# A second layer's condition computed with features on partitions: the adapters become the held operand, the squares are summed by a product with ones, and the normed rows are no longer transposed

## The chip, the core and the metric

The kernel runs on one core of a Trainium2 chip. The metric is the device time of one execution in microseconds (us). Five engines work beside each other, each through its own queue: TensorE (PE; its weight loads are listed as PEld), VectorE (DVE), ScalarE (ACT), GpSimd (POOL) and SyncE (SP, which here only issues transfers).

## The reference, cut to what matters

The input x has 8 groups of 128 rows with 512 features. Two layers are added to it one after the other, each a condition followed by a gated feed-forward block. Layer 0's condition is a base product with low-rank experts, and its block has 4-bit weights. Layer 1 is where most of the change lies:

```python
def _L1_cond_ref(x, weight, adapter_ids):
    w = weight[adapter_ids]                     # (8, 512, 512): one adapter for each group
    return jnp.einsum('bsi,boi->bso', x, w)

def _L1_ffn_ref(x, ln_w, gate_w, up_w, down_w):
    var = jnp.mean(jnp.square(x), axis=-1, keepdims=True)
    nx = x * jax.lax.rsqrt(var + RMS_EPS) * ln_w
    g = jnp.einsum('bsh,ih->bsi', nx, gate_w)
    u = jnp.einsum('bsh,ih->bsi', nx, up_w)
    return jnp.einsum('bsi,hi->bsh', jax.nn.silu(g) * u, down_w)

x = x + _L0_ffn_ref(_L0_cond_ref(x, ...), ...)
x = x + _L1_ffn_ref(_L1_cond_ref(x, L1_cond_weight, itok_B_3_7), ...)
```

For each of the 8 groups b, a (128 x 512) block of rows is multiplied by that group's own 512 x 512 adapter; every row is divided by its root mean square; every feature is multiplied by its weight `ln_w`; and the result is the input of 1792 gate and 1792 up columns.

## The kernel before, in words

All activations are kept with features on partitions: `xT` is 128 partitions x 4 chunks (KC) x 1024 rows. The gate, up and down products of both layers take their activations in that form. They don't run in plain float32: each operand is split into a high part, a low part and a scaled difference, written as float32r, and three cheaper products are added. For the activations of layer 1 these three are `a3[0]` (hi), `a3[1]` (lo) and `a3[2]` (di).

The condition of layer 1 does run in plain float32. `adapt(b)` (L995) computes group b with rows on partitions: `xT` is the held operand (lhsT), the adapter, 512 columns at a time, is streamed, and four products add up to 128 rows x 512 features in one bank of PSUM. A plain float32 product shows as two records of PE and two of PEld. ACT squares the bank and sums along the free axis in the same instruction (L1008; the sum shows as an ACTIVATION_READ_ACCUMULATOR record), takes the root of the 128 x 1 result (L1009), DVE inverts it (L1010) and multiplies the bank with it (L1012, `nx`). `normed(b, nx)` (L1015) then has TensorE turn the four 128 x 128 pieces (L1019, a product against the identity), DVE multiplies by `ln_w` on the way out of PSUM (L1023, `raw`), ACT writes the high part (L1030), and DVE the low part (L1031) and the difference (L1032).

The loop over the 8 groups calls `adapt(b)` and then `normed(b - 1)`. These instructions are not in a hand-written order: the framework's scheduler orders each engine's queue by the order of the program and by what it takes to be ready. The adapters are fetched by gathers on POOL's queue, 1 MB each, into three buffers; the fetch of group b + 3 is released by group b's last product. The preparation of the first two chunks of gate and up weights (L940, L943 on ACT; L949, L952 on DVE) is issued just before the loop.

What follows, and layer 0, is in a fixed order (`manual_schedule`): ACT, DVE and TensorE take their instructions as written. A small planner decides while the program is written which engine gets what. It keeps a clock that advances 0.2326 us for each product, and for ACT and DVE a time to which each is booked (`load`). `rescale` (L174) puts a pass over a PSUM bank on the engine whose booking would end earlier, and waiting tasks (weight preparation, splitting of h) are put in where they fit:

```python
def took(engine, n):
    return 0.1 + n / 1000 if engine == "act" else 0.15 + n / 950
...
engine = min(load, key=lambda e: max(load[e], clock[0] + AFTER) + took(e, n))
```

The first chunk of layer 1's gate and up products (`gate_up`, L1081) works on the first 512 rows alone; the last group's `normed` is issued in its middle, after the products of the first of the three parts (which = (2,)) and before the other two (which = (0, 1)), because groups 4 to 7 are needed only when the second 512 rows come. A gate or up bank is rescaled (L179 on ACT, L181 on DVE) between these two.

The activation tables: Sqrt and Silu are in different tables, so there is one table load (L1044) after the last root. After the layer's first rows there is also a one-row product that decides a flag (`judge`, L813), issued in the first `normed`.

Of the kernel before, what the change touches and what calls it, by code (L numbers as in the profile page):

```python
# [13 lines left out]
F32 = mybir.dt.float32  # L14
# [5 lines left out]
AF = mybir.ActivationFunctionType  # L20
ALU = mybir.AluOpType

P = 128
B, T, D = 8, 128, 512
# [4 lines left out]
KC = D // P  # L29
# [66 lines left out]
def network_in(ctx, tc, a, out, by_groups, flag, again):  # L96
    nc = tc.nc
# [4 lines left out]
    def pair(name):  # L102
        return psum.tile([P, 2, 512], F32, tag="ps", name=name)

    def bank(name):
        return pair(name)[:, 0, :]
# [15 lines left out]
    def behind(inst, other):  # L122

        info = mybir.DependencyInfo(mybir.DependencyClass.NoSync, mybir.DependencyReason.SCHED_ONLY)
        tc.add_manual_dep(inst.ins, other.ins.name, info, reason="order")
# [327 lines left out]
    def by_groups_of_scales():  # L453
# [243 lines left out]
        with tc.manual_schedule(engines={EngineType.PE, EngineType.DVE, EngineType.Activation}):  # L697
# [77 lines left out]
                for j in range(*pair0):  # L775
                    flush(f"w{j}")

            load["act"], load["dve"] = clock[0] + 1.0, clock[0] + 2.0

            queue_down(*BLOCKS0[0], "d0", at=clock[0] + 7.0)  # L780
            gate_up_pair(0, 1)
# [210 lines left out]

    last_root = [None]

    def adapt(b):  # L995
        ps = bank("adapt")
        wt = w1s.pop(b)
        for c in range(KC):
            nc.tensor.matmul(  # L999
                ps,  # L1000
                lhsT=xT[:, c, b * T : (b + 1) * T],
                rhs=wt[:, c * D : (c + 1) * D],
                start=(c == 0),
                stop=(c == KC - 1),
            )
        sq = ad.tile([P, D], F32, tag="t0", bufs=2, name="sq")
        ss = ad.tile([P, 1], F32, tag="ss", bufs=3, name="ss")
        nc.scalar.activation(sq, ps, AF.Square, accum_out=ss)  # L1008
        last_root[0] = nc.scalar.activation(ss, ss, AF.Sqrt, bias=eps, scale=1.0 / D)  # L1009
        nc.vector.reciprocal(ss, ss)  # L1010
        nx = ad.tile([P, D], F32, tag="t1", bufs=2, name="nx")
        nc.vector.tensor_scalar(nx, ps, ss, None, ALU.mult)  # L1012
        return nx

    def normed(b, nx):  # L1015
        both = pair("nxT")
        pt = both[:, 0, :]
        for c in range(KC):
            nc.tensor.transpose(pt[:, c * T : (c + 1) * T], nx[:, c * P : (c + 1) * P], ident)  # L1019
        if judges:  # L1020
            judges.pop()(both[:, 1, :])
        raw = ad.tile([P, KC, T], F32, tag="raw", bufs=2, name="raw")
        nc.vector.tensor_tensor(  # L1023
            raw,
            pt.rearrange("p (c t) -> p c t", c=KC),
            ln_w[:, :, None].to_broadcast([P, KC, T]),
            ALU.mult,
        )
        hi, lo, di = (x[:, :, b * T : (b + 1) * T] for x in a3)
        nc.scalar.activation(hi, raw, AF.Copy, scale=HSCALE)  # L1030
        nc.vector.tensor_tensor(lo, raw, hi.bitcast(F32), ALU.subtract)  # L1031
        nc.vector.scalar_tensor_tensor(  # L1032
            di, lo.bitcast(F32), -1.0 / EPS, hi.bitcast(F32), ALU.mult, ALU.add
        )

    prev = None
    for b in range(B):
        nx = adapt(b)
        if b + 3 < B:
            load_w1(b + 3)  # L1040
        if prev is not None:
            normed(b - 1, prev)
        prev = nx
    behind(nc.scalar.activation(root, root, AF.Silu), last_root[0])  # L1044


    w1_stack.close()
    f1 = ctx.enter_context(tc.tile_pool(name="f1", bufs=1, side="right"))
    load["act"], load["dve"] = clock[0] + 2.0, clock[0] + 1.0
    d3, h3 = {}, {}  # L1050

    def gu_sums(ps, j, half, tb, which):
# [132 lines left out]
    with tc.manual_schedule(engines={EngineType.PE, EngineType.DVE, EngineType.Activation}):  # L1185
        for j0, j1 in BLOCKS1:
            for j in range(j0, j1):
                if j + 2 < NJ1:
                    flush(f"w{j + 1}")
                    prepare(j + 2, f"w{j + 2}")  # L1190
                    if j + 4 < NJ1:
                        load_wgu(j + 4)
                flush(f"w{j}")
                if j == 0:

                    two = [begin_chunk(i) for i in range(2)]
                    first, second = slice(0, 1), slice(1, 2)
                    gate_up(two[0], first, between=lambda: normed(B - 1, prev))
                    ad_stack.close()
                    fd = ctx.enter_context(tc.tile_pool(name="fd", bufs=1, side="left"))  # L1200
                    gate_up(two[1], first)
                    gate_up(two[0], second)
                elif j == 1:
                    gate_up(two[1], second)
                else:
                    flush(f"h{j - 2}")
                    gate_up(begin_chunk(j))
                if j == max(j0, 1):
                    prepare_down(load_down(j0, j1))
            flush("down")  # L1210
            for j in range(j0, j1):
                flush(f"h{j}")
            if j1 == NJ1 and by_groups:

                again.append(nc.values_load(flag[:1, :], min_val=0, max_val=1))
                tc.mark_branch_hint_location("again", hint=again[0], engines=FETCHED)
            down(j0, j1)
# [158 lines left out]
```

## Time and profile before

| | |
|---|---|
| median of 3 runs | 436.3 us (435.57 to 436.6) |
| profiled execution | 436.83 us |
| its span, first to last instruction | 434.9 us |
| mean granted TensorE clock | 0.996 of full speed |
| busy: PE, PEld, DVE, ACT, POOL | 424.8, 334.5, 302.4, 232.0, 9.0 us |
| first adapt product (L999) to first layer-1 gate product (L1056) | 165.80 to 197.36 us |
| adapt products, 64 records | 28.9 us busy, 592 ns median of one |
| transposes (L1019), 32 records | 4.9 us busy, 272 ns median of one |

A line of a timeline gives: start in us from the beginning of the span, duration in us, engine, line of the program, instruction, written tile <- read tiles, shape (for a product: rows*columns of the held operand, then the streamed shape), count, and in brackets how long the engine was idle before and what ended that. Products of TensorE are pipelined: the duration of one includes its way through the array, so the pace is read from the distance between starts, not from durations. In the chain that ended last each share is the part of the span that a line or an engine carries on the way back from the last instruction.

### The profile page before, as it was taken

How to read it: one execution, taken by the hardware profiler on the slowest of the kernel's cores; microseconds unless marked ns; L12 is line 12 of the kernel's file. 1: busy time of each engine (PE TensorE's matmuls, PEld its weight loads, DVE VectorE, ACT ScalarE, POOL GpSimd, SP SyncE). 2: the span in 40 equal slices, each digit the busy share in tenths (PEclk: the TensorE clock that was granted, in tenths of full speed). 3: DMA queues.
4: the chain of work that ended last, by engine and by line, in shares of the span. 5: the costliest groups of instructions: out<-in, count | busy, mean ns of one | idle time of the engine just before them, and what ended most of it. 6: DMA issues, size and time to landing. Idle time of an engine off the chain costs nothing.

```text
span 434.9 us, 4847 instructions
## 1 busy us (share of the span) xinstructions
PE 424.8 (98%) x1855; PEld 334.5 (77%) x1855; DVE 302.4 (70%) x432; ACT 232.0 (53%) x269; POOL 9.0 (2%) x20
## 2 busy tenths in 40 slices
PE   8999999999999999999999999999999999999992
PEld 8875778888888764447888888888888888888882
DVE  3998979998998769768179634679334676725552
ACT  5923899678877765347478132484132471425420
POOL 1000000000002001100000000000000000000000
PEclk9999999999999999999999999999999999999998
DMA  8931301010001505842114101132001110000013
GB/s 290 344 150 49 98 0 50 18 37 2 0 2 48 242 6 204 301 167 83 64 50 145 48 2 48 50 97 72 2 0 48 50 48 26 0 0 2 2 53 146
DMA packets 12094, 33.07 MB, mean 76 GB/s; under 512 B 1568, under 2 KB 4256, under 8 KB 11040
## 3 DMA queue, kind: packets, MB, share of 16 engines
q1 hardware_dynamic: 9760, 22.21, 15.3%
q0 software_dynamic: 1152, 8.39, 5.1%
q10 hardware_dynamic: 1152, 2.10, 1.3%
q8 instruction: 16, 0.26, 0.2%
q14 instruction: 14, 0.11, 0.1%
HBM read 30.59 MB, written 2.10 MB: 75 GB/s over the span
## 4 chain that ended last, share of the span: by engine, by line
PE 91%; DVE 4%; DMA 2%; ACT 1%; issue 0%; SPq 0%; ACTq 0%; DVEq 0%
PE gate L1056 18%; PE up L1056 18%; PE down L1121 17%; PE gate L539 9%; PE down L587 8%; PE up L539 8%; PE base L390 5%; PE adapt L999 5%; PE base L416 2%; DMA xb<-in_xb 2%; PE experts L293 1%; DVE xT L599 1%; PE nxT L1019 1%; ACT sl L555 1%; DVE h L558 1%; DVE w L952 1%
## 5 line engine op out<-in xcount | busy, mean ns | idle before, releaser
L1056 PE MATMUL gate<-a,w 128*128 128x512 f32 x336 | 81.8, 390 | 0.0
L1056 PE MATMUL up<-a,w 128*128 128x512 f32 x336 | 81.4, 389 | 0.0
L1121 PE MATMUL down<-h,d 128*128 128x512 f32 x336 | 76.8, 389 | 0.0
L1056 PEld LDWEIGHTS up<-a,w 128*128 128x128 f32 x336 | 63.1, 188 | 13.2
L1121 PEld LDWEIGHTS down<-h,d 128*128 128x128 f32 x336 | 63.1, 188 | 13.1
L1056 PEld LDWEIGHTS gate<-a,w 128*128 128x128 f32 x336 | 62.7, 188 | 13.5 <-ACT gate L179 0.6
L1073 DVE SCALAR_TENSOR_TENSOR h<-up,sl 128x1024 f32<-128x1024 f32 (+1 forms) x16 | 17.5, 1092 | 51.0 <-PE up L1056 44.6
L539 PE MATMUL gate<-a,dq 128*128 128x512 f32 (+1 forms) x176 | 47.7, 393 | 0.1
L539 PE MATMUL up<-a,dq 128*128 128x512 f32 (+1 forms) x176 | 47.4, 391 | 0.0
L587 PE MATMUL down<-h,wd 128*128 128x512 f32 (+1 forms) x176 | 42.3, 393 | 0.6 <-DVE h L193 0.4
L587 PEld LDWEIGHTS down<-h,wd 128*128 128x128 f32 (+1 forms) x176 | 32.5, 188 | 9.5 <-DVE h L193 0.9
L539 PEld LDWEIGHTS gate<-a,dq 128*128 128x128 f32 (+1 forms) x176 | 32.4, 185 | 8.4 <-ACT sl L555 0.6
L539 PEld LDWEIGHTS up<-a,dq 128*128 128x128 f32 (+1 forms) x176 | 32.4, 185 | 7.9 <-DVE a L671 0.3
L203 ACT ACTIVATE h<-h 128x1024 fp32r<-128x1024 f32 (+1 forms) x25 | 26.4, 1054 | 15.9 <-DVE h L1073 15.5
L1070 ACT ACTIVATE sl<-gate 128x1024 f32<-128x1024 f32 (+1 forms) x16 | 14.7, 919 | 35.8 <-PE gate L1056 35.8
L193 DVE TENSOR_TENSOR h<-h,h 128x1024 fp32r<-128x1024 f32 (+1 forms) x25 | 30.5, 1218 | 3.4 <-ACT h L203 3.4
L179 ACT ACTIVATE gate<-gate,ratio 128x1024 f32<-128x1024 f32 (+1 forms) x24 | 26.1, 1086 | 10.6 <-PE gate L539 10.6
L179 ACT ACTIVATE gate<-gate 128x1024 f32<-128x1024 f32 (+1 forms) x15 | 13.8, 923 | 30.8 <-PE gate L1056 30.8
L999 PE MATMUL adapt<-w,xT 128*128 128x512 f32 x64 | 28.9, 597 | 0.0
L179 ACT ACTIVATE down<-down 128x1024 f32<-128x1024 f32 (+1 forms) x10 | 9.2, 923 | 35.8 <-PE down L1121 35.8
L179 ACT ACTIVATE up<-up,ratio 128x1024 f32<-128x1024 f32 (+1 forms) x23 | 25.0, 1085 | 4.9 <-PE up L539 4.9
L1138 DVE SCALAR_TENSOR_TENSOR xT<-down,xT 128x1024 f32<-128x1024 f32 (+1 forms) x17 | 19.6, 1161 | 9.3 <-PE down L1121 9.1
(137 smaller groups left out, 482.6 us busy)
## 6 DMA issues: line engine op xcount, KB each, us to landing
wgu<-in_wgu SPq DMA_DIRECT2D x14, 512.0 KB, 3.3
wd<-in_wd SPq DMA_DIRECT2D x6, 512.0 KB, 3.7
qw<-in_qw_gu SPq DMA_DIRECT2D x5, 512.0 KB, 4.2
xT<-in_xT SPq DMA_DIRECT2D x2, 1024.0 KB, 11.6
xb<-in_xb ACTq DMA_DIRECT2D x4, 256.0 KB, 5.6
xb<-in_xb SPq DMA_DIRECT2D x4, 256.0 KB, 6.1
wT<-in_WT SPq DMA_DIRECT2D x4, 256.0 KB, 5.9
qwd<-in_qw_d SPq DMA_DIRECT2D x2, 512.0 KB, 8.2
```

Of the source, the lines that this page charges most:

```text
L179: nc.scalar.activation(ps, ps, AF.Copy, scale=by)
L193: nc.vector.tensor_tensor(lo, x, hi.bitcast(F32), ALU.subtract)
L203: nc.scalar.activation(hi, x, AF.Copy, scale=HSCALE)
L390: nc.tensor.matmul(base[m], lhsT=wT3[i][:, m, c * P : (c + 1) * P], rhs=x_parts(tb)[i][:, c, :], start=(i == 0 and c == 0), stop=(i == 1 a ...
L539: nc.tensor.matmul(ps, lhsT=dqs[j][:, c, half, :], rhs=a3[i][:, c, tb * TB : (tb + 1) * TB], start=(c == 0 and i == 0), stop=(i == 1), ski ...
L587: nc.tensor.matmul(ps[:, tb], lhsT=wds[k][:n, m * P : (m + 1) * P], rhs=h2[k][i][:, tb], start=(first and i == 0), stop=(i == 1), skip_gro ...
L999: nc.tensor.matmul(ps, lhsT=xT[:, c, b * T : (b + 1) * T], rhs=wt[:, c * D : (c + 1) * D], start=(c == 0), stop=(c == KC - 1),)
L1056: nc.tensor.matmul(ps, lhsT=w3[j][i][:, c, half * P : (half + 1) * P], rhs=a3[i][:, c, tb * TB : (tb + 1) * TB], start=(i == 2 and c == 0) ...
L1070: nc.scalar.activation(sl, ps, AF.Silu, scale=1.0 + EPS)
L1073: nc.vector.scalar_tensor_tensor(h, ps, 1.0 + EPS, sl, ALU.mult, ALU.mult)
L1121: nc.tensor.matmul(banks[m, tb], lhsT=d3[j][i][:, m * P : (m + 1) * P], rhs=h3[j][i][:, tb], start=(i == 0 and j == j0), stop=(j == j1 - 1 ...
L1138: nc.vector.scalar_tensor_tensor(x, ps, -EPS, x, ALU.mult, ALU.add)
```

## The change

The condition of layer 1 is computed in the turned form at once. For each of the four 128-feature pieces m of the output, a 128 x 128 piece of the adapter is held and the group's 128 rows of `xT` are streamed, over four chunks c: 16 products of 128 columns in place of 4 of 512. The bank then holds features on partitions, 4 pieces x 128 rows, and needs no transposes. The sum of squares now runs over partitions and pieces: ACT squares the bank (no accumulator), DVE adds the four pieces (a strided `tensor_reduce`, 128 x 512 to 128 x 128), and TensorE multiplies the result with a 128 x 128 matrix of ones, which gives every partition the full sum for each row (`mean`, in the second bank of the same pair). Root and reciprocal are now taken of 128 x 128 elements. `ln_w` is per partition and goes into four scaled copies on ACT (`y`), and DVE multiplies `y` in place by the inverse root. High part, low part and difference are as before.

The mean, root and reciprocal of group b - 1 (`rooted`) are issued in the middle of group b's products, after two of its four pieces. For the last group `rooted`, the table load and `normed` are issued together in the middle of the first gate and up chunk. Two starting values of the planner's bookings change: ACT's at the start of layer 0's gate and up products from 1.0 to 2.0, DVE's at the start of layer 1's from 1.0 to 2.0.

```diff
-            load["act"], load["dve"] = clock[0] + 1.0, clock[0] + 2.0
+            load["act"], load["dve"] = clock[0] + 2.0, clock[0] + 2.0
...
-    def adapt(b):
-        ps = bank("adapt")
+    all_ones = ad.tile([P, P], F32, name="all_ones")
+    nc.gpsimd.memset(all_ones, 1.0)
+
+    def adapt(b, between):
+        both = pair("adapt")
+        ps = both[:, 0, :]
         wt = w1s.pop(b)
-        for c in range(KC):
-            nc.tensor.matmul(
-                ps,
-                lhsT=xT[:, c, b * T : (b + 1) * T],
-                rhs=wt[:, c * D : (c + 1) * D],
-                start=(c == 0),
-                stop=(c == KC - 1),
-            )
+        roots = None
+        for m in range(KC):
+            if m == KC // 2 and between is not None:
+                roots = between()
+            for c in range(KC):
+                nc.tensor.matmul(
+                    ps[:, m * T : (m + 1) * T],
+                    lhsT=wt[:, c * D + m * P : c * D + (m + 1) * P],
+                    rhs=xT[:, c, b * T : (b + 1) * T],
+                    start=(c == 0),
+                    stop=(c == KC - 1),
+                )
         sq = ad.tile([P, D], F32, tag="t0", bufs=2, name="sq")
-        ss = ad.tile([P, 1], F32, tag="ss", bufs=3, name="ss")
-        nc.scalar.activation(sq, ps, AF.Square, accum_out=ss)
-        last_root[0] = nc.scalar.activation(ss, ss, AF.Sqrt, bias=eps, scale=1.0 / D)
-        nc.vector.reciprocal(ss, ss)
-        nx = ad.tile([P, D], F32, tag="t1", bufs=2, name="nx")
-        nc.vector.tensor_scalar(nx, ps, ss, None, ALU.mult)
-        return nx
-
-    def normed(b, nx):
-        both = pair("nxT")
-        pt = both[:, 0, :]
-        for c in range(KC):
-            nc.tensor.transpose(pt[:, c * T : (c + 1) * T], nx[:, c * P : (c + 1) * P], ident)
+        ss = ad.tile([P, T], F32, tag="ss", bufs=2, name="ss")
+        y = ad.tile([P, KC, T], F32, tag="y", bufs=2, name="y")
+        nc.scalar.activation(sq, ps, AF.Square)
+        nc.vector.tensor_reduce(ss, sq.rearrange("p (m t) -> p t m", m=KC), mybir.AxisListType.X, ALU.add)
+        for m in range(KC):
+            nc.scalar.activation(y[:, m, :], ps[:, m * T : (m + 1) * T], AF.Copy, scale=ln_w[:, m : m + 1])
+        return (both, ss, y), roots
+
+    def rooted(got):
+        both, ss, _ = got
+        mean = both[:, 1, :T]
+        nc.tensor.matmul(mean, lhsT=all_ones, rhs=ss, start=True, stop=True)
         if judges:
-            judges.pop()(both[:, 1, :])
-        raw = ad.tile([P, KC, T], F32, tag="raw", bufs=2, name="raw")
-        nc.vector.tensor_tensor(
-            raw,
-            pt.rearrange("p (c t) -> p c t", c=KC),
-            ln_w[:, :, None].to_broadcast([P, KC, T]),
-            ALU.mult,
-        )
+            judges.pop()(both[:, 1, T:])
+        rms = ad.tile([P, T], F32, tag="rms", bufs=2, name="rms")
+        last_root[0] = nc.scalar.activation(rms, mean, AF.Sqrt, bias=eps, scale=1.0 / D)
+        nc.vector.reciprocal(rms, rms)
+        return rms
+
+    def normed(b, got, rms):
+        raw = got[2]
+        nc.vector.tensor_tensor(raw, raw, rms[:, None, :].to_broadcast([P, KC, T]), ALU.mult)
         hi, lo, di = (x[:, :, b * T : (b + 1) * T] for x in a3)
...
     for b in range(B):
-        nx = adapt(b)
+        got, rms = adapt(b, None if prev is None else lambda: rooted(prev))
         if b + 3 < B:
             load_w1(b + 3)
         if prev is not None:
-            normed(b - 1, prev)
-        prev = nx
-    behind(nc.scalar.activation(root, root, AF.Silu), last_root[0])
+            normed(b - 1, prev, rms)
+        prev = got
+
+    def last_row():
+        rms = rooted(prev)
+        behind(nc.scalar.activation(root, root, AF.Silu), last_root[0])
+        normed(B - 1, prev, rms)
...
-    load["act"], load["dve"] = clock[0] + 2.0, clock[0] + 1.0
+    load["act"], load["dve"] = clock[0] + 2.0, clock[0] + 2.0
...
-                    gate_up(two[0], first, between=lambda: normed(B - 1, prev))
+                    gate_up(two[0], first, between=last_row)
```

## The prediction

> **What bounds the kernel now.** I read the page first (engine shares, the chain that ended last), then the order of time around the rows of the condition, then single lines for durations.
>
> ```profile
> PE 424.8 (98%) x1855; PEld 334.5 (77%) x1855; DVE 302.4 (70%) x432; ACT 232.0 (53%) x269; POOL 9.0 (2%) x20
> PE 91%; DVE 4%; DMA 2%; ACT 1%; issue 0%; SPq 0%; ACTq 0%; DVEq 0%
> ```
>
> TensorE is the bound: it carries 91% of the chain. A microsecond of product taken away on it is worth one, unless a new wait takes its place. One steady row of the condition:
>
> ```profile
> 181.34 0.60 PE L1019 MATMUL nxT<-ident,nx 128*128 128x128 f32 x4
> 181.54 0.60 ACT L1008 ACTIVATE sq<-adapt 128x512 f32<-128x512 f32 x1 [2.08 <-PE adapt L999]
> 181.77 3.60 PE L999 MATMUL adapt<-w,xT 128*128 128x512 f32 x8
> 181.97 0.69 DVE L1023 TENSOR_TENSOR raw<-nxT,small 128x512 f32<-128x512 f32 x1 [0.99 <-PE nxT L1019]
> 182.03 0.20 ACT L1008 ACTIVATION_READ_ACCUMULATOR sq<-adapt 128x1 f32 x1
> 182.26 0.29 ACT L1009 ACTIVATE ss<-ss,eps 128x1 f32<-128x1 f32 x1
> 182.59 0.16 DVE L1010 RECIPROCAL ss<-ss 128x1 f32<-128x1 f32 x1
> 182.70 0.63 ACT L1030 ACTIVATE a<-raw 128x512 fp32r<-128x512 f32 x1
> 182.79 0.75 DVE L1012 TENSOR_SCALAR nx<-adapt,ss 128x512 f32<-128x512 f32 x1
> 183.45 0.68 DVE L1031 TENSOR_TENSOR a<-raw,a 128x512 fp32r<-128x512 f32 x1
> 184.17 0.69 DVE L1032 SCALAR_TENSOR_TENSOR a<-a,a 128x512 fp32r<-128x512 f32 x1
> 185.21 0.60 PE L1019 MATMUL nxT<-ident,nx 128*128 128x128 f32 x4
> ```
>
> From transposes to transposes a row lasts 3.87 us: 8 product records at 0.430 (3.44) and 4 transposes at 0.1075 (0.43). TensorE doesn't wait in it. DVE works 0.16+0.75+0.69+0.68+0.69 = 2.97 us of it, ACT 0.60+0.19+0.29+0.63 = 1.71. So 0.9 us a row is spare on DVE and 2.2 on ACT.
>
> Where the rows end and the gate and up products begin (first chunk):
>
> ```profile
> 200.74 0.63 ACT L1030 ACTIVATE a<-raw 128x512 fp32r<-128x512 f32 x1
> 201.28 1.05 ACT L940 ACTIVATE w<-wgu 128x1024 fp32r<-128x1024 f32 x1
> 202.23 0.57 ACT L1070 ACTIVATE sl<-gate 128x512 f32<-128x512 f32 x1
> 202.71 1.05 ACT L943 ACTIVATE wgu<-wgu 128x1024 f32<-128x1024 f32 x1
> 204.79 0.58 ACT L179 ACTIVATE gate<-gate 128x512 f32<-128x512 f32 x1 [1.04 <-PE gate L1056]
> 205.50 2.04 PE L1056 MATMUL gate<-a,w 128*128 128x512 f32 x8
> ```
>
> ACT goes here in the written order: the last row's high part (200.74), the next weights (201.28), the Silu, their second pass, then the gate rescale that TensorE needs for its products at 205.50. ACT had 1.04 us to spare before that rescale. Whatever makes the last row's high part over about 1 us later stops TensorE.
>
> **The change, part by part.**
>
> *Products.* Eight records of 512 columns become 32 of 128 a row; four transposes become two records of the mean. The streamed columns are the same (8x512 = 32x128). The price of a 128-column record is bounded by two rows: the transposes, 0.1075, and
>
> ```profile
> 8.25 4.90 PE L293 MATMUL experts<-wa,xb 128*128 128x136 f32 x40 [0.29 <-DMA xb<-in_xb]
> 12.90 0.48 PE L390 MATMUL base<-a,wT 128*128 128x512 f32 x1
> ```
>
> 40 records of 136 columns between 8.25 and 12.90, 0.116 each, every one with its own full-size weight load, as after the change. I take the experts row, the nearer in kind, times 128/136: 0.109. A row then costs 34x0.109 = 3.71 us against 3.87, 0.16 less; 3.66 to 3.94 by the two ends. Eight rows: -1.3 us (-1.7 to +0.6).
>
> The Trainium skill ("TensorE: Matmul & The Clock Gate", Back-to-back issue gap) speaks against the change: in a stream where every product has its own weight load, both set the spacing, about 81 ns where the product alone needs 56 at 128 columns. An estimate that stretches 0.1075 by that ratio has 0.156 a record, 5.3 us a row and some 11 us lost. The experts row, at 0.116 with loads between all its products, says otherwise.
>
> *DVE.* Gone: the norm multiply from PSUM (0.75) and the one-column reciprocal (0.16). New: a reduction over 512 elements, and a reciprocal over 128. The reduction's rows are 0.25 us for 93 elements (L693) and 0.68 for a 512-element pass (L1031); I take 0.69. Its strided read is in no row; I keep 0.6 to 1.2. For the reciprocal:
>
> ```profile
> L534 DVE RECIPROCAL ratio<-ratio x1: 566/566/566, 38.6 to 38.6; 128x66 f32<-128x66 f32 x1
> L534 DVE RECIPROCAL ratio_d<-ratio_d x1: 379/379/379, 41.8 to 41.8; 128x36 f32<-128x36 f32 x1
> ```
>
> 187 ns for 30 elements, 6.2 ns each: 128 cost 0.379+92x0.0062 = 0.95 us. DVE's row becomes 0.69+0.95+0.69+0.68+0.69 = 3.70 us, equal to TensorE's 3.71. The spare 0.9 us is gone.
>
> *ACT.* The square keeps 0.60 and loses its accumulator read (0.19). Four scaled copies of 128 columns come: the immediate-scale form is 0.58 at 512 and 1.01 at 1024 columns (L179), so 0.26 at 128; the pointer-scale form is 0.08 dearer (1.09 at 1024): 0.34, four make 1.36. The root grows from 1 to 128 elements: 0.29+127x0.00083 = 0.40. With the high part 0.63: 2.99 us a row. This hides under 3.71 while the order lets it; uncovered, the copies cost their 1.36.
>
> *The new wait.* TensorE now waits in the middle of each row for the reduction of the row before: 0.20 (product to ACT) + 0.60 + 0.05 + 0.69 + 0.06 = 1.60 us after that row's end, against a half row of 1.75. Behind the mean stand all further products. 0.15 us of slack is less than any DVE instruction (0.64 to 0.95) that happens to be ahead of the reduction. If DVE, at 3.70 plus three hand-offs of 0.05, sets the pace, it is 0.14 a row, 1.1 us; if TensorE needs only the reductions and DVE's rest may lag, nothing. I take +0.6 us.
>
> *First row.* DVE is in weight preparation until 171.25 (L949), so the first mean is possible at about 172.0; before, the first transposes waited as well (173.22 instead of 172.93). Nothing, from -0.3 to +1.
>
> *Last row.* Let E be the end of the last adapt products. Now (E = 197.01) the last high part ends at 201.37, 4.4 after. After the change: square to E+0.8, copies to 2.16, the gate rescale (moved to ACT, below) to 2.74, then the root (the mean is done at 1.82+0.22) to 3.14. The table load and its dummy, 1.28+0.20, end at 4.62, under DVE's reciprocal and multiply; these two end at 3.2+0.95+0.69 = 4.84 if DVE is free, about 6.5 if it still has row 6's 1.6 us. So the high part ends between 5.5 and 7.2. From there 1.05+0.57+1.05+0.58 = 3.25 us of ACT to the end of the gate rescale: E+8.8 to 10.4. TensorE without a stall wants it at E + 1.82 + 0.22 + 3.64 + 1.82 = E+7.5. The stall is 1.3 to 2.9; now it is 205.50 - 197.01 - 8.14 = 0.35 (8.14 being the products and two sets of transposes). Net +1.0 to +2.6; I take +2.3, since row 6's work does stand ahead now too (its last two parts run at 201.95 and 202.67).
>
> *The planner's constants.* Layer 1: by its own costs the gate rescale was 1.92 on DVE and 2.61 on ACT, and is now 2.69 and 2.61; so gate goes to ACT and up to DVE, the reverse of before (counted above). Layer 0: with ACT booked one later, the first "up" goes to DVE (3.91 against 4.25) and ACT has eight rescales of the first pair instead of nine. TensorE's only stalls there are 0.34 us at 45.84 and 0.56 at 58.06, both of other causes; the planner's books meet again in the second pair. Nothing, -0.2 to +0.3. The ones tile is set by idle POOL.
>
> *Sum.* -1.3 products, +0.6 row waits, 0 first row, +2.3 last row, 0 planner: +1.6 us. On the profiled execution (span 434.9, 436.83 with the 1.93 around it) that is 438.4; its own time stands 0.5 above the median of the runs, 436.3, so the median goes to 437.9.
>
> **The rivals.**
> 1. *Faster: the waits hide.* If the copies of the first half run during the second half of the products, ACT is 0.7 us earlier at the end and the high part ends near E+5.0; the last-row stall is 0.75, net +0.4. With no row waits: -1.3+0.4 = -0.9, with the cheap record -1.3: 435.0 to 435.4. For it: 2.2 us of ACT were spare, DVE idles later (2.45 us before 209.47). Against: DVE at 3.70. It decides where the last high part ends before about E+5.2.
> 2. *Much slower: DVE is held in the written order*, reciprocal, reduction, multiply, then a wait for the high part (0.05+0.63+0.07), low part, difference: 3.70+0.75 = 4.45 a row, +0.58 on seven rows = 4.1, with the last row's 2.3: 442.7. Half of the rows so: about 440. For it: low and difference need the high part, which now queues behind four copies. Against: before, the scheduler moved the multiply (181.97) ahead of the next reciprocal.
> 3. *Adapter loads late.* The gathers are issued 0.5 us after a row's end and land in 5.4 to 7.3; two rows from now are 7.6. At most 0.2 a row, 1 us in all: about 438.5.
>
> **How the numbers follow.** The forecast, 436.7 to 439.5, has 0.47; rival 1 0.32; rival 2 0.16; rival 3 0.05. A difference of 0.2%, 0.9 us, is about what can be told from no change. Of the forecast 0.07 lies within it, of rival 1 0.05; so faster 0.27, same 0.12, slower 0.61. The range has to reach into rival 1 and half of rival 2: 434.9 to 441.0.
>
> **What would show it.** Right: adapt records near 0.109 apart, reciprocal near 0.95, gate rescale on ACT, and a TensorE wait of over 1 us ahead of the second chunk's gate products. Wrong: a reciprocal under 0.4 us (then DVE has its slack back), records at 0.15, or no wait there.

## The result, and the profile after

The changed kernel takes 440.17 us (median of 6 runs, 439.05 to 441.66) against 436.41 us for the kernel before (6 runs): the ratio is 1.0083, with a 95% interval of 1.0069 to 1.0097. It is 3.8 us slower, where 1.6 was forecast. The profiled execution took 439.05 us with a span of 437.3, the shortest of its six runs.

From the page of the changed kernel: busy time by engine, and the engines' shares of the chain that ended last.

```profile
PE 425.4 (97%) x2031; PEld 349.9 (80%) x2031; DVE 309.9 (71%) x432; ACT 239.4 (55%) x293; POOL 9.5 (2%) x21
...
PE 93%; DVE 4%; ACT 1%; issue 1%; ACTq 0%; DVEq 0%
```

TensorE is still the bound, but DVE has 309.9 us of work where it had 302.4, and the page now lists its reciprocal (L1033) with 1% of the chain. Which stage lost the time is read from busy times by window. Two windows are shown: the eight rows of the condition, from the first adapt product to the first gate product of layer 1, and the first two chunks on the first 512 rows. Columns: window, its length, then busy us and instructions of PE, PEld, DVE, ACT, POOL, the granted clock, the DMA share and GB/s. First the kernel before:

```profile
165.80:197.36 31.56, 31.27 (x95) 14.96 (x95) 24.36 (x40) 14.48 (x32) 4.89 (x5) 1.00 0.54 200
197.36:209.20 11.84, 11.84 (x55) 9.37 (x54) 8.45 (x12) 8.09 (x14) 0.00 (x0) 1.00 0.40 134
```

and the changed kernel:

```profile
165.15:198.74 33.59, 32.01 (x274) 30.87 (x273) 30.62 (x40) 21.11 (x52) 5.20 (x5) 1.00 0.54 190
198.74:211.54 12.80, 12.02 (x54) 9.24 (x52) 9.79 (x13) 8.98 (x17) 0.00 (x0) 1.00 0.34 122
```

The rows take 33.59 us in place of 31.56 (+2.03), the first two chunks 12.80 in place of 11.84 (+0.96), layer 0, from its first gate product to the first adapt product, 123.37 in place of 123.20 (+0.17), and what follows the two chunks is the same (225.8 and 225.7). That is 3.16 us. The spans differ by only 2.4 because this execution reached layer 0's first gate product 0.82 us earlier (41.78 against 42.60), a moment that lies between 41.7 and 43.1 in all profiles shown here, of either kernel. In the rows TensorE is idle for 1.6 us by these busy times, before for 0.3, and DVE is busy for 30.62 of 33.59 us, before for 24.36 of 31.56.

One steady row of the changed kernel, in order of time (DVE's low part at 188.57, ACT's root at 188.96, DVE's difference at 190.23 and ACT's high part at 192.24 are among the lines left out):

```profile
188.46 0.46 PE L1028 MATMUL adapt<-ss,all_ones 128*128 128x128 f32 x2 [0.32 <-DVE ss L1019]
...
188.75 3.74 PE L1008 MATMUL adapt<-xT,w 128*128 128x128 f32 x32
...
189.36 0.95 DVE L1033 RECIPROCAL rms<-rms 128x128 f32<-128x128 f32 x1
...
190.74 0.60 ACT L1018 ACTIVATE sq<-adapt 128x512 f32<-128x512 f32 x1 [1.42 <-PE adapt L1008]
190.77 0.68 DVE L1038 TENSOR_TENSOR y<-y,rms 128x512 f32<-128x512 f32 x1
191.24 1.14 ACT L1021 ACTIVATE y<-adapt,small 128x128 f32<-128x128 f32 x4
191.37 1.05 DVE L1019 TENSOR_REDUCE ss<-sq 128x128 f32<-128x512 f32 x1
...
192.54 0.30 PEld L1028 LDWEIGHTS adapt<-ss,all_ones 128*128 128x128 f32 x2 [0.24 <-ACT y L1021]
...
192.92 0.69 DVE L1041 TENSOR_TENSOR a<-y,a 128x512 fp32r<-128x512 f32 x1 [0.50 <-ACT a L1040]
```

The mean's records start at 188.46 and again at 192.57: a row lasts 4.11 us, before 3.87. Two closed chains have this length. Along the first, mean to square takes 2.28 (mean, half a row of products, the hand-off to ACT), the square and its hand-off 0.63, the sum over the pieces (L1019) 1.05, the hand-off to TensorE 0.15: together 4.11. Along the second, DVE does low part, reciprocal, difference, multiply, sum (0.69 + 0.95 + 0.63 + 0.68 + 1.05 = 4.00), and its next low part waits for the high part (0.50 us at 192.92), which stands behind the four copies of `y` on ACT. This chain takes two rows to close: mean to square 2.28, square to the end of the high part 2.16, the hand-off 0.02, low part to the end of the sum 3.67 (a little under 4.00, since the records overlap), the hand-off 0.14, together 8.27 us from the mean at 188.46 to the one at 196.73, or 4.13 a row. The multiply ends at 191.45 and the square at 191.34, so the sum at 191.37 is released by both at about the same time. The wait hardly shows on the product's own line: it stands on the mean's weight load at 192.54 (0.24). The line names the copies as what ended it, but they end at 192.38 and the sum at 192.42, and from the second row on every mean of this kernel starts 0.15 us after its sum and 0.19 or more after its copies.

### The profile page after: what moved, and what is told of

Same layout as the page of the kernel before. It is cut to its first block, busy times and chain, and to the rows that moved or that the text cites. A ratio compares the mean times of both kernels' runs of the same rounds, so it can differ in the third digit from the quotient of the medians.

```text
span 437.3 us, 5236 instructions
## 1 busy us (share of the span) xinstructions
PE 425.4 (97%) x2031; PEld 349.9 (80%) x2031; DVE 309.9 (71%) x432; ACT 239.4 (55%) x293; POOL 9.5 (2%) x21
## 3 DMA queue, kind: packets, MB, share of 16 engines
HBM read 30.59 MB, written 2.10 MB: 75 GB/s over the span
## 4 chain that ended last, share of the span: by engine, by line
PE 93%; DVE 4%; ACT 1%; issue 1%; ACTq 0%; DVEq 0%
PE down L1135 17%; PE gate L1070 17%; PE up L1070 17%; PE gate L539 9%; PE down L587 9%; PE up L539 9%; PE base L390 5%; PE adapt L1008 5%; PE experts L293 2%; PE base L416 2%; PE idle L246 1%; PE adapt L1028 1%; DVE rms L1033 1%; DVE h L558 1%; ACT sl L555 1%
## 5 line engine op out<-in xcount | busy, mean ns | idle before, releaser
L1008 PE MATMUL adapt<-xT,w 128*128 128x128 f32 x256 | 30.1, 276 | 0.0
L179 ACT ACTIVATE gate<-gate,ratio 128x1024 f32<-128x1024 f32 (+1 forms) x22 | 23.9, 1086 | 10.5 <-PE gate L539 10.5
L179 ACT ACTIVATE up<-up,ratio 128x1024 f32<-128x1024 f32 (+1 forms) x24 | 26.1, 1086 | 6.4 <-PE up L539 6.4
L1008 PEld LDWEIGHTS adapt<-xT,w 128*128 128x128 f32 x256 | 29.2, 192 | 0.4 <-DVE xT L599 0.4
```

Of the source, the lines that this page charges most:

```text
L179: nc.scalar.activation(ps, ps, AF.Copy, scale=by)
L1008: nc.tensor.matmul(ps[:, m * T : (m + 1) * T], lhsT=wt[:, c * D + m * P : c * D + (m + 1) * P], rhs=xT[:, c, b * T : (b + 1) * T], start=( ...
```

## The experiments

All are compared with runs of the kernel before on the same chip (medians 436.4 to 436.8). "Rows" is from the first adapt product to the first gate product of layer 1, "chunks" from there to the first gate product of the second 512 rows; both from the one profiled execution. After, e8 and e9 have the same rows and show 33.59, 33.17 and 33.65, so a difference under half a microsecond in the rows column is not resolved.

| kernel | median us | ratio to before, 95% | rows us | chunks us |
|---|---|---|---|---|
| before | 436.41 | | 31.56 | 11.84 |
| after | 440.17 | 1.0083, 1.0069 to 1.0097 | 33.59 | 12.80 |
| e1_contig | 440.26 | 1.0077, 1.0063 to 1.0091 | 33.98 | 13.09 |
| e2_ones4 | 440.11 | 1.0074, 1.0060 to 1.0087 | 33.44 | 12.85 |
| e3_late | 439.61 | 1.0063, 1.0049 to 1.0077 | 32.82 | 13.45 |
| e4_short | 438.70 | 1.0047, 1.0033 to 1.0062 | 33.44 | 12.25 |
| e5_adds_own | 438.37 | 1.0040, 1.0027 to 1.0054 | 32.85 | 12.84 |
| e6_late_adds | 438.48 | 1.0047, 1.0034 to 1.0061 | 30.71 | 13.95 |
| e7_late_pool | 437.30 | 1.0016, 1.0006 to 1.0027 | 30.59 | 12.87 |
| e8_dve1 | 439.76 | 1.0079, 1.0064 to 1.0094 | 33.17 | 12.73 |
| e9_after_w2 | 439.21 | 1.0065, 1.0053 to 1.0077 | 33.65 | 12.25 |
| e10_best | 436.76 | 1.0007, 0.9995 to 1.0020 | 31.99 | 11.78 |
| e11_before_w2 | 436.38 | 0.9999, 0.9989 to 1.0008 | 31.45 | 11.83 |
| e12_before_act2 | 436.45 | 1.0004, 0.9995 to 1.0013 | 31.40 | 11.80 |

### The strided read of the sum (e1_contig)

```diff
-        nc.scalar.activation(sq, ps, AF.Square)
-        nc.vector.tensor_reduce(ss, sq.rearrange("p (m t) -> p t m", m=KC), ...)
+        nc.scalar.activation(sq.rearrange("p (t m) -> p m t", m=KC), ps.rearrange("p (m t) -> p m t", m=KC), AF.Square)
+        nc.vector.tensor_reduce(ss, sq.rearrange("p (t m) -> p t m", m=KC), ...)
```

> The squares are written with the four pieces of a row beside each other, so that DVE's sum over pieces reads contiguously (after the change it reads at a stride of 512 bytes and takes 1.05 us). Theory A (DVE's work of 4.0 us a row sets the pace of 4.13): if the stride is what makes the sum dear, it takes 0.69, DVE's row is 3.65, the pace falls to TensorE's 3.8 and the kernel gains 7 x 0.33 = 2.3 us. Theory B (TensorE's own records, 34 at 0.112 and the gap at each mean, are the pace): nothing changes, within 0.3 us. Theory C (the stride costs nothing, the sum is 1.05 for another reason): the sum stays 1.05 and the time with it.

Measured: no gain. Four lines of a row's timeline:

```profile
191.10 1.13 ACT L1018 ACTIVATE sq<-adapt 128x512 f32<-128x512 f32 x1 [1.42 <-PE adapt L1008]
...
192.03 1.08 ACT L1021 ACTIVATE y<-adapt,small 128x128 f32<-128x128 f32 x4
192.26 0.69 DVE L1019 TENSOR_REDUCE ss<-sq 128x128 f32<-128x512 f32 x1 [0.28 <-ACT sq L1018]
...
193.17 0.49 PE L1028 MATMUL adapt<-ss,all_ones 128*128 128x128 f32 x2 [0.31 <-ACT y L1021]
```

The sum falls from 1.05 to 0.69, but the square, which now writes with a stride, grows from 0.60 to 1.13. The 0.36 us are real and belong to the stride, and moving the stride to ACT moves the price with it. The row gets longer (mean at 188.79 and 193.17, 4.38) because the copies stand behind the square: the mean starts 0.06 us after they end at 193.11. That is a third condition on the mean. It is written into the second bank of the pair whose first bank the copies read, and the profile names the copies as what releases it.

### The sum taken from DVE altogether (e2_ones4)

```diff
-        nc.vector.tensor_reduce(ss, sq..., ALU.add)
...
-        nc.tensor.matmul(mean, lhsT=all_ones, rhs=ss, start=True, stop=True)
+        for m in range(KC):
+            nc.tensor.matmul(mean, lhsT=all_ones, rhs=sq[:, m * T : (m + 1) * T], start=(m == 0), stop=(m == KC - 1))
```

The square and the ones are written as float32r, so that each of the four products is one record.

> DVE's sum over the four pieces is left out; TensorE adds the four pieces of squares itself by four products with ones (squares and ones in float32r, one record each) in place of one float32 product (two records). DVE's row is 2.95 us. Theory A: the pace falls to TensorE's, 32 x 0.112 + 4 x 0.06 to 0.11 = 3.8 to 4.0 a row, a gain of 1 to 2.3 us, and more at the last row, whose chain loses 1.05. Theory B: the row gains nothing or loses up to 0.2.

Measured: no gain in time. With 1.05 us of DVE gone from every row, the row is 4.21:

```profile
191.50 1.13 ACT L1021 ACTIVATE y<-adapt,small 128x128 f32<-128x128 f32 x4
...
192.68 0.66 PE L1029 MATMUL adapt<-sq,all_ones 128*128 128x128 f32 x4
```

The copies run from 191.50 to 192.63 and the mean starts at 192.68. So the sum isn't the only thing in its place: without it the copies hold the mean, and the mean itself has grown from two records to four (0.50 against 0.30 between its start and the next product). DVE's time alone isn't the cause of the slower rows.

### The mean behind all products of a row (e3_late)

```diff
-            if m == KC // 2 and between is not None:
-                roots = between()
...
+        if between is not None:
+            roots = between()
         sq = ad.tile([P, D], F32, tag="t0", bufs=2, name="sq")
```

> The mean of the row before is issued after all 16 products of a row instead of after 8, so the sum has 1.8 us more time. Theory A (DVE's throughput): the pace stays at 4.1 and the time within 0.5 us. Theory D (only the latency from square to mean misses the half row): TensorE no longer waits, the pace falls to 3.8 and the kernel gains about 2.3 us. Theory B: no change.

Measured: a gain of 0.6 us by the medians, with overlapping intervals. The two last means, on PE's timeline:

```profile
197.66 0.46 PE L1028 MATMUL adapt<-ss,all_ones 128*128 128x128 f32 x2 [1.32 <-DVE ss L1019]
...
200.94 0.49 PE L1028 MATMUL adapt<-ss,all_ones 128*128 128x128 f32 x2 [0.97 <-ACT y L1021]
```

With a whole row of products to hide it, the first chain is broken: where no adapter is late, rows follow at 3.80 us (means at 188.58 and 192.38). But DVE, whose row is 4.00 us of work, falls behind, and the two last means pay for it: 1.32 us of wait for the sum, and 0.97 for the copies, which stand on ACT behind a high part that had waited 1.17 us for DVE. This shows that the second chain is real, and separate from the first.

### DVE relieved without touching the first chain (e4_short)

```diff
-        nc.vector.reciprocal(rms, rms)
+        nc.vector.reciprocal(rms[:, :1], rms[:, :1])
```

> The reciprocal is taken of one column instead of 128 (0.16 us instead of 0.95); the inverse is left out for the other columns. DVE's row is 3.2 us. Theory A: the pace falls to 3.8, a gain of 2.3 us in the rows, and up to 0.8 more at the last row, where the reciprocal stands in the chain to the second chunk's gate rescale. Theory D: the way from square to mean has no reciprocal in it, so the rows stay within 0.5 us; only the last row gains up to 0.8. Theory B: as D.

The inverse of the other 127 columns is left out here.

Measured: 1.5 us less than after, but the steady rows do not get shorter:

```profile
191.28 1.05 DVE L1019 TENSOR_REDUCE ss<-sq 128x128 f32<-128x512 f32 x1 [0.54 <-ACT sq L1018]
...
192.47 0.46 PE L1028 MATMUL adapt<-ss,all_ones 128*128 128x128 f32 x2
```

The reciprocal falls to 0.15 us and DVE has time to spare (it waits 0.54 us for the square before the sum), and yet the row is 4.11 (the mean before starts at 188.36): the first chain alone, with the same 2.29, 0.63, 1.05 and 0.14. Relieving DVE pays at the end: the wait before the second chunk's gate products is gone, and the chunks are 0.55 us shorter. This profile also has a wait of 0.90 us for a late adapter, which the rows stage of 33.44 contains; without it the stage would be about 1 us shorter than after, in the rows ahead of the steady ones.

### Both chains shortened (e5_adds_own, e6_late_adds)

```diff
-        nc.vector.tensor_reduce(ss, sq..., ALU.add)
+        half = ad.tile([P, 2 * T], F32, tag="half", bufs=2, name="half")
+        nc.vector.tensor_tensor(half, sq[:, : 2 * T], sq[:, 2 * T :], ALU.add)
+        nc.vector.tensor_tensor(ss, half[:, :T], half[:, T:], ALU.add)
```

Two additions of contiguous pieces take 0.42 + 0.29 us on DVE where the strided sum took 1.05. In e5 the mean also gets a pair of banks of its own (`both = pair("mean")`), which frees it from the copies; in e6 it goes behind all products, as in e3.

> Two edits: the sum over four pieces is made by two contiguous additions on DVE (256 and 128 columns; 0.42 + 0.28 = 0.70 us where the strided sum takes 1.05), and the mean gets a pair of PSUM banks of its own instead of the second bank of the pair whose first bank the four copies read. Theory E (in the changed kernel the mean waits for whichever ends later of the sum and the four copies of the same row; the copies hold it only because they share its pair): the mean starts while the copies still run, 1.66 us after a row's end, inside the half row of 1.79; TensorE no longer waits and the row is 0.30 + 32 x 0.112 = 3.88, a gain of 7 x 0.25 = 1.7 us. Theory A (DVE's throughput): 3.65 a row, so the pace falls as well, to 3.88; the mean still starts after the copies. Theory F (the copies' data are not what holds it, only DVE is): as A. The trace decides between E and A: the start of the mean against the end of the copies.

> The mean is issued after a row's 16 products, as in the run before of that kind, and the sum is two contiguous additions (0.70 us instead of 1.05). With the late mean alone the rows ran at 3.79 until DVE, behind by then, held the last two means for 1.3 and 1.0 us. Theory G (two limits beside each other: the latency from square to mean for the mean in the middle, and DVE's work for the end of the stage): rows at 3.79, no wait over 0.3 at the last means, a gain of 2 to 3 us on the changed kernel: about level with the kernel before. Theory A alone: the same. Theory E alone (only the copies matter): no better than the late mean by itself (0.6 us gained).

Measured: both gain 1.7 to 1.8 us on after. In e5 one row is 3.81 us, after a late adapter that had left DVE 0.90 us of idle time, and the next 4.15: there DVE waits 0.73 us for the high part, and its multiply then stands ahead of the additions. Its rows stage contains 1.12 us of waiting for that adapter. As to the pair of banks: one mean of e5 (192.68) starts 0.15 us after its sum and 0.03 us before its copies end, while in the versions that share the pair no mean starts less than 0.05 us after its copies (e1 and e2 at just that distance). This speaks for theory E's coupling, but it is one row of one profile. In e6 the rows are at 3.80 us but for the first (3.89) and one of 4.02, but at the end DVE is late again: 1.39 us before the last mean and 0.75 before the second chunk's gate products, so the chunks take 13.95.

### The sum on GpSimd (e7_late_pool)

```diff
-        nc.vector.tensor_tensor(half, ...); nc.vector.tensor_tensor(ss, ...)
+        nc.gpsimd.tensor_tensor(half, ...); nc.gpsimd.tensor_tensor(ss, ...)
```

> As the run with late mean and two additions, but the additions go to GpSimd, idle till now but for the gathers, so that DVE's row is 2.95 us. Theory G: rows at 3.79 and the last means without a wait, a gain of 2.5 to 3.5 us on the changed kernel, and better than with the additions on DVE by up to 1. If GpSimd's additions take over 1.5 us or slow DVE beside them, or delay the gathers behind them, the gain is less or none.

Measured: 437.30, of the loss 0.7 us is left. The mean's records and the waits of PE in the stretch:

```profile
189.25 0.39 PE L1030 MATMUL adapt<-ss,all_ones 128*128 128x128 f32 x2
...
193.04 0.39 PE L1030 MATMUL adapt<-ss,all_ones 128*128 128x128 f32 x2
```

```profile
PE gate L1072 <- ACT gate L179: 0.8, 1, 0.8
PE adapt L1030 <- POOL ss L1021: 0.3, 1, 0.3
```

These are the only two waits of the stretch: none is in the rows, which take 3.79 us for 32 products and a mean, 30.59 for the stage, 0.97 less than before (0.34 of it product time, the rest less waiting). GpSimd is slower (0.73 to 1.01 us and 0.45 or more), but idle. What is left is in the chunks: 0.28 and 0.78 us of wait.

### The planner's second constant (e8_dve1)

```diff
-    load["act"], load["dve"] = clock[0] + 2.0, clock[0] + 2.0
+    load["act"], load["dve"] = clock[0] + 2.0, clock[0] + 1.0
```

> Only the second planner constant is taken back (DVE's booking at the start of layer 1's gate and up products 1.0 instead of 2.0), so the first gate rescale goes back to DVE and the first up rescale to ACT. Theory of the last row (ACT's written order sets the second chunk's gate rescale): ACT has the same number of instructions, the up rescale stands behind the gate's place, so within 0.5 us. If the first gate rescale on ACT behind the copies is what costs the 0.39 us of wait at the first chunk, 0.3 to 0.5 us are gained.

Measured: inconclusive in time (1.0079 against 1.0083). The trace shows an exchange: the wait before the first chunk's gate products is gone, the one before the second chunk's is 0.56 instead of 0.34.

### ACT's order at the end (e9_after_w2, e10_best, e11_before_w2)

```diff
-        weights(w3[j], wgus.pop(j), name)
+        weights(w3[j], wgus.pop(j), name, at=clock[0] + 8.0 if j == 2 else 0.0)
```

The third chunk's two weight passes on ACT (L940, L943) come 8 us later, behind the second chunk's gate rescale. e9 is the changed kernel with it, e10 is e7 with it, e11 the kernel before with it.

> The changed kernel, with the third chunk's weights (w2) queued 8 us later, so that ACT does the Silu and both rescales of the second chunk before the two weight passes. Theory (tail): in the changed kernel TensorE waits 0.34 us before the second chunk's gate products because the gate rescale stands behind the first weight pass, the Silu and the second pass; with the passes moved behind it the wait goes to nothing, the rescale ends before the second chunk's up products do, and the time falls by 0.3 to 0.4 us, to about 439.8. Rival (the tail is not ACT's order but the last row's own latency): the wait stays, the time stays at 440.2. The wait before the last mean (0.29) and the one before the first chunk's gate products (0.39) stay under both.

> The version with the mean behind all sixteen products of a row and the sum of squares as two additions on GpSimd (437.3 us, 1.0016 of the kernel before), and w2 queued 8 us later on ACT. Its two waits at the chunks were 0.28 (last mean, for GpSimd's sum) and 0.78 (second chunk's gate products, for the gate rescale behind w2's two passes). Theory (tail): the 0.78 goes, since the last high part ends at 203.18, Silu 0.58 and rescale 0.59 end near 205.2 and TensorE is ready at 205.31: 436.5, ratio 0.9998 (0.998 to 1.001); the rows stage stays 30.6 us, 0.97 shorter than before, the two chunks fall from 12.87 to 12.1. Rival (the time is given back later, at the next chunk, because w2's passes now stand before the second half's gate rescale): the wait at 206.09 goes but one of 0.5 or more comes near 211, and the time stays 437.3.

> Control: the kernel before, with the same later w2. It has a wait of 0.35 us before the second chunk's gate products, with the same weight passes ahead of the Silu and the rescale. Theory (tail): 0.3 us less than the kernel before, 436.1, ratio 0.9993; so of the gain of the version with late mean and GpSimd, about 0.3 would be open to the kernel before too. Rival: no change (ratio 1.0000 +- 0.0005), because a later wait takes it back.

Measured: the wait before the second chunk's gate products is gone in both versions with the turned condition, and the chunks fall by 0.55 (12.80 to 12.25) in e9 and by 1.09 (12.87 to 11.78) in e10. The medians fall by 1.0 and 0.5 us, with overlapping intervals. Two lines of e10's end, after one of its rows:

```profile
194.42 3.84 PE L1006 MATMUL adapt<-xT,w 128*128 128x128 f32 x32 [0.47 <-DMA w<-in_w,row]
...
205.64 0.58 ACT L179 ACTIVATE gate<-gate 128x512 f32<-128x512 f32 x1 [0.91 <-PE gate L1072]
...
206.35 2.02 PE L1072 MATMUL gate<-a,w 128*128 128x512 f32 x8
```

The last high part starts at 203.61, the Silu at 204.15, and the gate rescale follows as soon as its products are done and ends at 206.22; the products start at 206.35 without a wait. The chunks are then as short as before (11.78, 11.84). In the kernel before the same edit brings nothing (0.9999): there was no wait to take away, and the 0.35 us that the prediction had taken for one isn't in its trace.

e10 is the best version with the turned condition, and the only one that isn't measurably slower than the kernel before: 1.0007, from 0.9995 to 1.0020. It isn't faster either. Its profile shows where the 0.97 us of e7's rows can go: TensorE waits 0.47 us at 194.42 for an adapter (gathers take 6.9 to 8.0 us from issue to landing there, and two rows of 3.80 are 7.6), and the first rows took 0.6 us more than in e7's. In e7's profile the gathers took 5.6 to 6.3 us and there was no such wait.

### The planner's first constant alone (e12_before_act2)

```diff
-            load["act"], load["dve"] = clock[0] + 1.0, clock[0] + 2.0
+            load["act"], load["dve"] = clock[0] + 2.0, clock[0] + 2.0
```

> The kernel before with only the first planner constant of the change (ACT booked one later in layer 0, 2.0 for 1.0). The prediction's step: nothing, -0.2 to +0.3 us, so 436.3 to 436.8 against 436.5. Rival: this constant is the unseen part of the loss, +0.5 us or more, through a rescale that lands on the wrong engine in layer 0's first chunks; then the trace shows a TensorE wait of that size between 42 and 60 us that the kernel before does not have.

Measured: 1.0004, 0.9995 to 1.0013. From layer 0's first gate product to the first adapt product its profile has 123.38 us, as the changed kernel (123.37), where the kernel before has 123.20 and e11 123.22. All twelve profiles that have the constant lie between 123.33 and 123.42, the two without it at 123.20 and 123.22. It shows as one longer distance between two products' starts (0.38 us here, 0.40 after, where the pace is 0.23) about 18.5 us after layer 0's first gate product, which neither the kernel before nor e11 has. So the constant costs about 0.17 us, too little for the medians.

## Why the prediction was right, and where its sizes were wrong

The direction held, and 440.17 lies in the range (434.9 to 441.0). But it lies above the forecast itself (436.7 to 439.5), in the part of the range that had been added for half of rival 2: the change cost 3.8 us where the sum had 1.6. That it came so near is in part luck, since two errors partly cancelled: the rows were 2.8 us dearer and the end 1.3 us cheaper than forecast, so the main loss wasn't where the forecast had put it:

| term | predicted | in the profiles |
|---|---|---|
| products of the rows | -1.3 | -0.3 |
| row waits, first row included | +0.6 | +2.4 |
| last row and first chunks | +2.3 | +0.96 |
| planner's constant in layer 0 | 0 | +0.17 |
| sum | +1.6 | +3.2 |

The first two lines split the stage like this. After, 256 adapt records at 0.1118 (the pace between starts inside a group of 32: 3.74 less the last record's 0.275, over 31) and seven means of two records are 30.2 of 33.59 us, so 3.4 is not product. Before, 64 records at 0.430 and 28 transposes at 0.1075 are 30.5 of 31.56, so 1.0 is not. (The last row's mean and transposes lie in the chunks' line.) The medians differ by 3.8; the 0.6 above the sum isn't resolved by one profile of each. Late adapters, which cost 0.2 to 1.1 us in six of the variants' profiles (e1, e3, e4, e5, e9, e10) and nothing in this one, are a candidate, not shown.

*Products.* 0.109 a record was expected, 0.1118 measured: within the bounds, but a row without waits is then 34 x 0.1118 = 3.80 us (e7 shows just that), 0.07 less than 3.87 and not 0.16. The Trainium skill ("TensorE: Matmul & The Clock Gate", Back-to-back issue gap), by the estimate drawn from it, would have had 0.156; the trace does not agree with that estimate for these float32 products of 128 columns, each with its own weight load.

*DVE's row.* The reciprocal was right (0.95). The sum was not: 0.69 was taken, 1.05 measured. The bounds of 0.6 to 1.2 held it, but they were carried neither into DVE's row nor into the new wait. A rule of the Trainium skill that the prediction passed over points the right way: by "SBUF — State Buffer" (Door 1: The DMA port swizzle, the note on cachelines) an access that crosses to a new line of 16 bytes pays a penalty. The runs agree in direction on both sides: every element a new line costs 0.36 us per 512 read by DVE (1.05 against 0.69), and 0.52 per 512 written by ACT (1.12 against 0.60). No run varies the stride, so that the lines are the cause is not shown.

*The new wait, the step that failed.* The chain from a row's last product to the mean was put at 1.60 us against half a row of 1.75, "0.15 us of slack". It is 2.03 (0.20 + 0.63 + 1.05 + 0.15) against 1.79. With a sum of 1.05 the same formula gives 1.96, a wait in every row, about 1.5 us in seven: the number that decides the step was the one that no row of the trace showed. The step also looked at one chain. e2, e3 and e4 show that three conditions close at nearly the same moment (the sum behind the square, the sum behind DVE's other work, the copies), so that taking any one away brings 0.8 us or less in the rows stage (about 1.0 in e3 and e4 if their late adapters are left out), and taking two away (e6, e7) brings the rows to 3.80.

*Rival 2* (DVE held in the written order, 4.45 a row) described the second chain, and got a chance of only 0.16 because the scheduler had moved a multiply before. A part of it came true: DVE does wait 0.26 to 0.50 us in each steady row for a high part behind four copies. Its "about 440" for half of the rows is the time that was measured, but not by that way: the steady rows take 4.11 to 4.16 us with 4.00 of DVE's work, not some 4.45 and some 3.71. *Rival 1* would have needed slack in both chains. *Rival 3*, late adapters, is not in the changed kernel's trace; it appears in variants whose rows are shorter or come at another time.

*The last row.* The mechanism is the one described, and its size was off. PE and ACT of the changed kernel at the end (left out between: weight pass 204.77, Silu 205.72, second pass 206.19):

```profile
201.71 2.11 PE L1070 MATMUL gate<-a,w 128*128 128x512 f32 x8 [0.39 <-ACT gate L179]
...
204.23 0.63 ACT L1040 ACTIVATE a<-y 128x512 fp32r<-128x512 f32 x1 [0.78 <-DVE y L1038]
...
207.14 0.59 ACT L179 ACTIVATE gate<-gate 128x512 f32<-128x512 f32 x1
...
207.78 1.43 PE L1070 MATMUL gate<-a,w 128*128 128x512 f32 x5 [0.34 <-ACT gate L179]
```

The last high part, the weight pass, the Silu, the second pass and the gate rescale follow each other as forecast, the gate rescale on ACT, and end at 207.73. The last product ended 0.20 before its square at 199.02, so that is E + 8.9, inside the forecast E + 8.8 to 10.4. But TensorE wanted the rescale later than E + 7.5, having waited about 0.2 us for the last mean (0.44 between its start and that of the product before it, where the pace is 0.23) and 0.39 us before 201.71, where the first chunk's gate rescale stands behind the high part of row 6. So only 0.34 is left for the place where over 1 us was expected. All three together are about 0.95. The kernel before has no wait there, so nothing was to be deducted for it: the "0.35 now" was spread over hand-offs in the whole stretch.

*The planner's constant.* The stalls of 0.34 us at 45.84 and 0.56 at 58.06 that the prediction reads as TensorE's are idle times of the weight loads; by the starts of the products about 0.1 and 0.3 us are lost there. The constant's own 0.17 (e12) was put at nothing, inside its bounds of -0.2 to +0.3.

*First row.* TensorE was idle for 0.51 us before the first mean, before it 0.29 ahead of the first transposes: +0.2, as close as "nothing" can be taken.

Of the four signs that the prediction named, records near 0.109, the reciprocal near 0.95 and the gate rescale on ACT came; the wait of over 1 us before the second chunk did not.

## What to carry to other kernels

A step that passes a small result through three engines in the middle of a product stream is free only while that round trip has slack: add up the whole closed chain, with both ends of each unknown duration, and do so for every engine that has to keep the pace. When several chains close within 0.3 us of each other, removing one shows almost nothing, so undo two at a time before calling a suspect innocent. A pass that is moved to a less busy engine (GpSimd here) or behind more products can repair a round trip, but what it gains in the rows is then limited by the next thing that was sized for the old pace, here the order of ACT at the end and, in e10's profile, an adapter gather.

## What the runs showed of the hardware that was not expected

- Summing four pieces with a stride of 128 float32 elements: 1.05 us for 512 to 128 elements, 0.69 when the four lie side by side, 0.42 + 0.29 as two additions of contiguous pieces. On ACT a write at a stride of four elements costs more as well: the square of 512 elements 1.12 us against 0.60.
- Four scaled copies of 128 columns on ACT take 1.14 us together: each shows 0.37, but they start 0.25 apart. The 1.36 of the prediction was too much.
- GpSimd needs 0.73 to 1.01 us for an addition of 256 columns that DVE does in 0.42, and 0.45 to 0.96 (1.3 once) for one of 128 that DVE does in 0.29. DVE's passes beside them are a little longer: its multiply 0.75 us on average in e7's rows where it has 0.68 in e6's, and one weight pass 1.63 where it has 1.22.
- 128-column float32 products with a weight load each run at 0.1118 us a record, a little faster than the 136-column ones of layer 0 (0.116) and slower than the transposes (0.1075). The mean, a pair of such records, starts its second record 0.185 us after the first where it had to wait, and 0.112 where it had not (e7).
